# A bias added to four transposed chunks in one instruction, and a gate's mix issued one iteration later

## The chip, the cores and the metric

The kernel runs on one core of a Trainium2 chip. The metric is the device time of one execution in microseconds. A core has five engines that run side by side, each through its own list of instructions in order: TensorE (PE in the profile; its weight loads are shown apart as PEld), VectorE (DVE), ScalarE (ACT), GpSimd (POOL), and SyncE (SP), which here only issues transfers. A row whose engine ends in q (ACTq, DVEq) belongs to that engine's sequencer: a branch, a register read or the issue of a transfer.

## The reference, cut to what matters

The program is two layers. The first is a mixture of experts over tokens, and then a feed-forward network whose weights are chosen per sequence; the second mixes each token with the one before it, sends it to an expert and gates the result, and ends in a recurrent network. The stage that the change touches does the per-sequence network of layer one and the mixing and gate of layer two, for 32 sequences of 128 tokens with 512 features:

```python
sel = jnp.argmax(action_probs, axis=-1)          # one of 8 experts for each sequence
h = gelu(einsum('bsh,bhf->bsf', hidden_states, W1[sel]) + b1[sel][:, None, :])
reasoned = einsum('bsf,bfh->bsh', h, W2[sel]) + b2[sel][:, None, :]
x = ... hidden_states + 0.3 * (reasoned @ Wo + bo)
# second layer
xprev = concatenate([shift_state[:, None, :], x[:, :-1]], axis=1)
xk = x + (xprev - x) * time_maa_k                # goes to the experts
xr = x + (xprev - x) * time_maa_r                # goes to the gate
r = sigmoid(einsum('btd,ed->bte', xr, w_recept))
```

## The kernel before, in words

Everything is fp32 with each matrix operand held as two numbers, a high and a low part. `split(hi, lo, src)` makes them: a cast on ScalarE (L63) and a subtract on VectorE (L64). A product is then three matmuls, (high, high), (high, low) and (low, high), which `mm3` (L71) issues for each of four chunks of the contraction, so one product of 128 tokens by 512 columns is twelve matmuls.

The stage runs from about 862 us to 1466 us of the span. The sequences are sorted by expert, so that neighbours share weights. Weights are gathered on the GpSimd queue into three raw buffers (`fetch_w`, `rawB`, L851), with the biases of a sequence (L858) beside them; `split_w` (from L866) splits one of the four halves W1a, W2a, W1b, W2b in two pieces of 128x1024, at run time only where the expert differs from that of the sequence before. A branch on a register (L879) decides that, on ScalarE and on VectorE. In the profiled data the splits run around iterations 6, 15 and 16, 26, and always at 24, where the second part of the sorted list begins.

An iteration b carries three sequences at different depths. In program order it does:

- `up(b+1, "a")`: twelve matmuls into `pu`, and a copy `ue` on ScalarE (L1021).
- `turn_r(b-1)`: the result `ps` of the sequence before the current one is transposed in four chunks (`pr`, L1052) into a PSUM tile. Then, for each chunk, ScalarE adds the bias and writes the high part `rT` (L1057), and VectorE adds the bias and subtracts the high part to get the low one (L1058). These eight instructions alternate, since each low part needs its high part.
- `down(b, "a")` into `po`.
- In some iterations a `combine` of the layer's token experts (transposes `pth`, ScalarE's `o` at L744, VectorE's `xc` at L749); after iteration 17 also the choice of experts for the second part, `policy`.
- `bend(b+1, "a")`: four transposes `pt` (L1028), four gelu activations `hf` with the bias (L1031), and the split `hb`.
- `send_k(pair)`: four transposes `ptB` of the mixed `xk` (L1130), a copy `rows` (L1132), and a transfer by SP. This, and the other steps for a pair, happen in every other iteration.
- `up(b+1, "b")`, `send_k(pair + 1)`, `down(b, "b")` with the copy `ps` (L1045), `send_v(pair)` (twelve matmuls `pv` of the gate on `xr`, a copy `r` at L1142 and a transfer), `bend(b+1, "b")`, `send_v(pair + 1)`.
- After every second sequence `close(c)`: the output product `pb` for the pair (48 matmuls of 256 columns), and on VectorE the sum `x` (L1095), the difference `dx` (L1078) and the mix `xk` (L1080). GpSimd first puts the shifted-in row into `x` (L1071, `x<-condS`).
- Directly after `close(c)`, `mix_r(c)`: four instructions on VectorE that turn `dx` into the gate's mix in place (L1116), and its split into `xr` (a cast and a subtract of 128x1024).

Text such as "iteration 16" below means the stretch from `pu_16a`'s first matmul to that of the next sequence, by the number in the name of the `pu` that begins it. `close` thus stands at the end of an odd stretch and its VectorE work runs into the even one that follows.

The order in which each engine issues is fixed when the kernel is built: a scheduler places the instructions by readiness and by the program's order, and `tc.issue_after(ins)` keeps what is issued inside it behind an instruction on that instruction's engine. A tile belongs to a pool, and a new tile waits until the tile that had its buffer has been read. The pool `ps_tB` has two PSUM buffers, and `pr`, `pt`, `ptB` and `pth` take turns in it. `ps`, `dx`, `xk`, `xr`, `x1` and `rT` have one buffer each, the biases four, `hb` three.

Of the kernel before, what the change touches and what calls it, by code (L numbers as in the profile page):

```python
# [1 line left out]

# [6 lines left out]
F32 = mybir.dt.float32  # L9
# [5 lines left out]
AF = mybir.ActivationFunctionType  # L15
ALU = mybir.AluOpType
# [4 lines left out]
P = 128  # L21
D = 512
KD = D // P
NB = 32
# [16 lines left out]
BIAS = {"W1a": 0, "W1b": 1, "W2a": 2}  # L41
# [7 lines left out]
def tile_kernel(ctx: ExitStack, tc: tile.TileContext, a: dict, out: bass.AP):  # L49


    nc = tc.nc
# [4 lines left out]
    def shifted(pool, n, by=SHIFT, **kw):  # L57

        return pool.tile([P, n + (LINE if by == SHIFT else by)], FR, **kw)[:, by : by + n]

    def split(hi, lo, src):

        nc.scalar.copy(hi, src)  # L63
        return nc.vector.tensor_tensor(lo, src, hi.bitcast(F32), ALU.subtract).ins  # L64

    def mm3(ps, left, right, kd, start=True, stop=True):

# [78 lines left out]
    with ExitStack() as sa:  # L146
# [696 lines left out]
        raws, bcol, changed = {}, {}, {}  # L843
# [16 lines left out]
                        in_offset=bass.IndirectOffsetOnAxis(ap=idxb[:, b : b + 1], axis=0),  # L860
                    )

        def bias_of(kind, b, o):
            return bcol[b][:, BIAS[kind] * KD + o : BIAS[kind] * KD + o + 1]

        def split_w(i):  # L866

# [18 lines left out]
        with ExitStack() as s2:  # L886
# [15 lines left out]
            for g in range(h, NG):  # L902
                own = list(range((g - 1) * GB, g * GB)) if g > h else []
                for c in range(KF):
                    n = (2 if 0 < c < 3 else 0) if g == last else 1
# [43 lines left out]
    with ExitStack() as sb:  # L949
        kw = dict(reuse_waits="tile")  # L950
        lp = sb.enter_context(tc.tile_pool(name="lp", bufs=2, **kw))
        bp = sb.enter_context(tc.tile_pool(name="bp", bufs=1, **kw))
# [11 lines left out]
        PB = 2  # L964
        HF = F1 // 2

        def weight_b(name):
            pair = wb.tile([P, 2, KD, D], FR, tag=name, name=f"{name}_hl")
            flat = pair.rearrange("p h k n -> p h (k n)")
            given = a[name].rearrange("p k n -> p (k n)")  # L970
            for q, tag in enumerate(("dx", "xk")):
                s = bass.ts(q, KD * D // 2)
                raw = bp.tile([P, KD * D // 2], F32, tag=tag, name=f"raw_{name}{q}")
                nc.sync.dma_start(out=raw, in_=given[:, s])
                split(flat[:, 0, s], flat[:, 1, s], raw)
            return pair

        seqs, end_p = {}, None
# [13 lines left out]
        rTs, xks, xrs = {}, {}, {}  # L992

        def fetch_hid(b):
            if b < NB:
                hid_raw[b] = lp.tile([P, KD, P], F32, tag="hid", name=f"hidB_{b}")
                nc.sync.dma_start(out=hid_raw[b].rearrange("p k q -> p (k q)"), in_=by_seq(hid_d, b))
# [4 lines left out]
        def fetch_xh(c):  # L1002
            if c < NB // PB:
                xs[c] = lp.tile([P, PB, KD, P], F32, tag="x", bufs=1, name=f"xB_{c}")
                for j in range(PB):
                    nc.sync.dma_start(
                        out=xs[c][:, j].rearrange("p k q -> p (k q)"), in_=by_seq(xh_d, c * PB + j)
                    )

        def split_hid(b):  # L1010
            if b < NB:
                raw = hid_raw.pop(b)
                hid_hl[b] = lp.tile([P, 2, KD, P], FR, tag="hidhl", name=f"hidhl_{b}")
                split(hid_hl[b][:, 0], hid_hl[b][:, 1], raw)

        def up(b, half):
            w = ws["W1" + half]
            pu = ps_u.tile([P, HF], F32, tag="u", name=f"pu_{b}{half}")
            mm3(pu, lambda h, k: hid_hl[b][:, h, k, :], lambda h, k: w[:, h, k, :], KD)
            ues[b, half] = rp.tile([P, HF], F32, tag="ue", name=f"ue_{b}{half}")  # L1020
            nc.scalar.copy(ues[b, half], pu)  # L1021
# [13 lines left out]
        def down(b, half):  # L1035
            w, hb = ws["W2" + half], hbs.pop((b, half))
            if half == "a":
                pos[b] = ps_o.tile([P, D], F32, tag="o", name=f"po_{b}")
            mm3(
                pos[b], lambda h, k: hb[:, h, k, :], lambda h, k: w[:, h, k, :], KD,  # L1040
                half == "a", half == "b",
            )
            if half == "b":
                pss[b] = rp.tile([P, D], F32, tag="ps", bufs=1, name=f"ps_{b}")
                nc.scalar.copy(pss[b], pos.pop(b))  # L1045

        def turn_r(b):
            c, j = divmod(b, PB)
            ps = pss.pop(b)
            pt = ps_t.tile([P, KD, P], F32, tag="t", name=f"pr_{b}")  # L1050
            for o in range(KD):
                nc.tensor.transpose(pt[:, o, :], ps[:, bass.ts(o, P)], ident)  # L1052
            if j == 0:
                rTs[c] = rTp.tile([P, 2, KD, PB * P], FR, tag="rT", name=f"rT_{c}")
            for o in range(KD):
                hi = rTs[c][:, 0, o, bass.ts(j, P)]
                done_a = nc.scalar.activation(hi, pt[:, o, :], AF.Identity, bias=bias_of("W2a", b, o))  # L1057
                done_v = nc.vector.scalar_tensor_tensor(  # L1058
                    rTs[c][:, 1, o, bass.ts(j, P)], pt[:, o, :], bias_of("W2a", b, o),
                    hi.bitcast(F32), ALU.add, ALU.subtract,  # L1060
                )
            return done_a.ins, done_v.ins

        def close(c, last=False):

# [46 lines left out]
        def mix_r(c, pool, tag):  # L1112

            _, dx, x1 = xks[c]
            for k in range(KD):
                nc.vector.scalar_tensor_tensor(  # L1116
                    dx[:, k], dx[:, k], maa_r[:, k : k + 1], x1[:, k, :, 1:], ALU.mult, ALU.add
                )
            if pool is not end_p:
                xrs[c] = pool.tile([P, 2, KD, PB, P], FR, tag=tag, name=f"xr_{c}")  # L1120
            else:
                xr = shifted(pool, 2 * KD * PB * P, LINE - SHIFT, tag=tag, name=f"xr_{c}")
                xrs[c] = xr.rearrange("p (h k b q) -> p h k b q", h=2, k=KD, b=PB)
            split(xrs[c][:, 0], xrs[c][:, 1], dx)
# [26 lines left out]
        def used():  # L1151
            nonlocal at
            split_w(at + AHEAD)
            at += 1

        for b in range(-1, NB + 1):
            c, j = divmod(b - 1, PB)
            if b + 1 < NB:
                up(b + 1, "a")
                used()  # L1160
                split_hid(b + 2)
                fetch_hid(b + 3)
            if 0 <= b - 1 < NB:
                r_done = turn_r(b - 1)
            if 0 <= b < NB:
                down(b, "a")
                used()
            if b == -1:
                fetch_xh(0)
            if b == 0:  # L1170
                wo0 = weight_b("Wo")
            if b == 1:
                wrec = weight_b("w_recept")

            late, step = divmod(b - 3, 3)
            if 0 <= late < GB and step == 0:
                get_o(NB - GB + late, cb, 1)
            if 0 <= late < GB and step == 2:
                combine(NB - GB + late, ps_t)
            if late == GB and step == 2:  # L1180
                policy(PARTS[0], NB, cb, ps_t)
            if b + 1 < NB:
                bend(b + 1, "a")

            pair = b - 3 if b % 2 and 0 <= b - 3 < NB - 2 else None
            if pair is not None:
                send_k(pair)
            if b + 1 < NB:
                up(b + 1, "b")
                used()  # L1190
            if late == GB and step == 2:
                sc.close()
                end_p = sb.enter_context(tc.tile_pool(name="end_p", bufs=1, **kw))
            if pair is not None:
                send_k(pair + 1)
            if b == NB:
                send_v(NB - 6)
            if 0 <= b < NB:
                down(b, "b")
                used()  # L1200
            if pair is not None and pair < NB - 6:
                send_v(pair)
            if b + 1 < NB:
                bend(b + 1, "b")
            if pair is not None and pair < NB - 6:
                send_v(pair + 1)
            if j == PB - 1 and 0 <= c < NB // PB:
                wo_done, k_done = close(c, b == NB)
                fetch_xh(c + 1)
                if c < NB // PB - 2:  # L1210
                    mix_r(c, bp, "xr")
                elif c == NB // PB - 2:
                    mix_r(c, end_p, "xr")

        with tc.issue_after(wo_done):
            send_v(NB - 5)
# [13 lines left out]
    with ExitStack() as sd:  # L1230
# [97 lines left out]
        for p in range(NPC):  # L1328
# [6 lines left out]
            if p == NPC - 12:  # L1335
                c = first_p.tile([P, D], F32, tag="c0", name="c_0")
                nc.sync.dma_start(out=c, in_=a["in_c"].partition_broadcast(P))
                cT = first_p.tile([P, 2, KD, P], FR, tag="cT0", name="cT_0")
                pt = ps_t.tile([P, KD, P], F32, tag="t", name="ptC_0")
# [25 lines left out]
    with sf:  # L1365
# [135 lines left out]
        ps, wx = {}, {}  # L1501
# [15 lines left out]
        bias = {n: load_row("b" + n, D, keep_p) for n in "cif"}  # L1517

        cT_next = cT
        for t in range(NB):  # L1520
# [15 lines left out]
            c = new_c(t, v, c)  # L1536
            ps = {}
# [58 lines left out]
        for n, (g, o) in enumerate(units):  # L1596
            if g == NG - 1:
                to_z(o)
                src = pos.pop(o)
                h = yp.tile([P, GT], F32, tag="y", name=f"hF_{g}_{o}")  # L1600
            else:
                src = h = zos[g, o]
# [99 lines left out]
```

## Time and profile before

| what | value |
|---|---|
| time, median of 3 runs | 2541.81 us (2541.47, 2541.81, 2545.81) |
| the profiled execution | 2535.17 us |
| its span, first to last instruction | 2533.5 us |
| mean granted TensorE clock | 0.988 |
| TensorE busy | 2460.9 us (97%) |
| VectorE busy | 1332.4 us (53%) |
| ScalarE busy | 1064.2 us (42%) |
| the stage of the change, 862 to 1466 us: TensorE busy | 590.31 of 604.00 us |

The profile is of one execution, and its own time stands above beside its span. "Busy" is time in which an engine executes something that computes. A row of the groups gives the line, the engine, the operation, what is written from what, the shape and count, then the busy time and the mean of one in ns, and then the idle time of that engine just before the group, with what ended it. In the chain of waits each engine's wait is put down to the instruction that released it. A "granted clock" below 1.00 means that TensorE's matmuls ran slower in part of the stretch.

### The profile page before, as it was taken

The numbers are of one execution on the slowest core, as the hardware profiler recorded it, in microseconds if no ns is written. First come the engines' busy times: TensorE is split into PE (matmuls) and PEld (weight loads), VectorE is DVE, ScalarE is ACT, GpSimd is POOL, SyncE is SP. The second block draws the span as 40 slices with busy tenths as digits, with TensorE's granted clock in tenths as the row PEclk, the third lists the DMA queues.
The fourth block names the chain that finished last, engine by engine and source line by source line (L and its number), as shares of the span: only waits on it lengthen the run. The fifth ranks groups of instructions, "written<-read, shape, count | busy, mean of one in ns | idle before, by whom it ended". The sixth has DMA issues, their size and how long they took to land. (4 is left out here: it accounts for less than half of the span.)

```text
span 2533.5 us, 37051 instructions
## 1 busy us (share of the span) xinstructions
PE 2460.9 (97%) x13044; PEld 2077.8 (82%) x13044; DVE 1332.4 (53%) x2341; ACT 1064.2 (42%) x1935; POOL 428.5 (17%) x460
## 2 busy tenths in 40 slices
PE   8999999999999899999999999999999999999996
PEld 6788899887887787888887889999978888888885
DVE  7796645556557344445444477667643333333336
ACT  5445533443224445445455466666532222222214
POOL 1000022222223223322322110000010000000003
PEclk9999999999999999999999999999999999999998
DMA  5545544557555333332243387776441111111027
GB/s 181 162 132 172 172 156 152 169 184 254 180 177 169 113 97 126 113 116 99 85 143 116 105 283 238 230 229 224 152 162 42 38 38 38 38 42 46 25 78 267
DMA packets 193116, 351.11 MB, mean 139 GB/s; under 512 B 37472, under 2 KB 72336, under 8 KB 189856
## 3 DMA queue, kind: packets, MB, share of 16 engines
q1 hardware_dynamic: 141504, 244.42, 29.0%
q0 software_dynamic: 36160, 74.90, 10.0%
q10 hardware_dynamic: 15264, 29.37, 3.3%
q8 instruction: 108, 1.77, 0.3%
q14 instruction: 80, 0.66, 0.1%
HBM read 373.94 MB, written 88.13 MB: 182 GB/s over the span
## 5 line engine op out<-in xcount | busy, mean ns | idle before, releaser
L64 DVE TENSOR_TENSOR wD<-rawD,wD 128x1024 fp32r<-128x1024 f32 x128 | 156.5, 1229 | 77.7 <-ACT wD L63 77.7
L71 PE MATMUL p<-xhl,swu 128*128 128x512 f32 x768 | 189.0, 397 | 5.3 <-ACT xhl L63 5.3
L71 PE MATMUL p<-xhl,kept_u 128*128 128x512 f32 x768 | 185.6, 397 | 0.7 <-DVE kept_u L64 0.7
L71 PEld LDWEIGHTS phD<-xe,wD 128*128 128x128 f32 x1536 | 184.7, 189 | 1.8 <-ACT xe L63 0.6
L71 PE MATMUL phD<-xe,wD 128*128 128x256 f32 x1536 | 185.7, 281 | 0.5 <-ACT xe L63 0.5
L71 PE MATMUL poD<-wD,hD 128*128 128x512 f32 x768 | 181.3, 392 | 0.0
L71 PEld LDWEIGHTS p<-xhl,swu 128*128 128x128 f32 x768 | 144.7, 191 | 36.5 <-ACT xhl L63 5.6
L71 PEld LDWEIGHTS p<-xhl,kept_u 128*128 128x128 f32 x768 | 143.3, 190 | 30.5 <-DVE kept_u L64 1.1
L71 PEld LDWEIGHTS poD<-wD,hD 128*128 128x128 f32 x768 | 141.9, 188 | 28.4
L63 ACT CAST wD<-rawD 128x1024 fp32r<-128x1024 f32 x128 | 133.2, 1047 | 53.6 <-PE poD L71 31.0
L266 POOL DMA_INDIRECT xg<-in_x_rows_dram,blk_t x71 | 67.5, 951 | 461.3 <-PE ptx L276 257.4
L1384 POOL DMA_INDIRECT y<-res_d,gat_i x32 | 32.2, 1005 | 575.0 <-DVE r L1403 496.2
L71 PE MATMUL pur<-r,xb 128*128 x852 | 117.8, 287 | 0.9 <-ACT xb L63 0.4
L71 PE MATMUL por<-r,hbr 128*128 x426 | 116.3, 407 | 1.2 <-ACT hbr L63 1.1
L64 DVE TENSOR_TENSOR xb<-ptx,xb 128x512 fp32r<-128x512 f32 x71 | 49.1, 691 | 115.3 <-ACT xb L63 113.7
L71 PEld LDWEIGHTS pur<-r,xb 128*128 128x128 f32 x852 | 104.9, 189 | 2.0 <-ACT xb L63 0.9
L71 PE MATMUL acc<-kept_d,as 128*128 128x512 f32 x384 | 96.1, 400 | 5.1 <-DVE as L64 3.1
L71 PE MATMUL poF<-z,wo_hl 128*128 128x512 f32 x384 | 96.5, 399 | 0.0
L71 PE MATMUL ps_f<-wf_hl,z 128*128 128x512 f32 x384 | 96.4, 399 | 0.0
L71 PE MATMUL ps_c<-wc_hl,z 128*128 128x512 f32 x384 | 94.9, 395 | 0.7 <-issue 0.7
L71 PE MATMUL acc<-swd,as 128*128 128x512 f32 x384 | 95.0, 392 | 0.0
L71 PE MATMUL pb<-rT,Wo_hl 128*128 128x256 f32 x768 | 94.6, 281 | 0.0
(1014 smaller groups left out, 5040.0 us busy)
## 6 DMA issues: line engine op xcount, KB each, us to landing
rawD<-in_w_key_dram SPq DMA_DIRECT2D x64, 512.0 KB
rawD<-in_w_value_dram SPq DMA_DIRECT2D x64, 512.0 KB
swr<-in_sw_dram SPq DMA_DIRECT2D x120, 256.0 KB
o_d<-obr SPq DMA_DIRECT2D x71, 256.0 KB
xraw<-in_x_dram SPq DMA_DIRECT2D x32, 256.0 KB
rraw<-in_rw_dram SPq DMA_DIRECT2D x32, 256.0 KB
xc<-in_x_dram SPq DMA_DIRECT2D x32, 256.0 KB
hid_d<-o ACTq DMA_DIRECT2D x32, 256.0 KB
```

Of the source, the lines that this page charges most:

```text
L63: nc.scalar.copy(hi, src)
L64: return nc.vector.tensor_tensor(lo, src, hi.bitcast(F32), ALU.subtract).ins
L71: done = nc.tensor.matmul(ps, lhsT=left(hl, k), rhs=right(hr, k), start=start and k + n == 0, stop=stop and 3 * k + n == last,)
L266: nc.gpsimd.indirect_dma_start(out=xg[i], out_offset=None, in_=a["x_rows"], in_offset=bass.IndirectOffsetOnAxis(ap=blk_t[:, i : i + 1], ax ...
L1384: nc.gpsimd.indirect_dma_start(out=y, out_offset=None, in_=res_d, in_offset=bass.IndirectOffsetOnAxis(ap=gat_i[:, b : b + 1], axis=0),)
```

## The change

Two things are edited, and a helper is added for the second. In `turn_r` the bias is added to all four transposed chunks by one VectorE instruction, which reads the PSUM tile and writes over the `ps` tile, whose content has been transposed by then; the bias operand is the sequence's four columns, each broadcast over 128 tokens. One `split` of the sum then writes the high and low parts of all four chunks. `split` now records its two instructions in `last_split`.

The mix for the gate, `mix_r(c)`, is no longer issued right after `close(c)` but in the following iteration after `bend(b+1, "a")`, and kept behind that bend's split `hb` on both ScalarE and VectorE. For one pair, at the end of the stage, no sequence is left to bend, and no such order is asked for. The last pair's mix stays where it was, after the loop.

```diff
     def split(hi, lo, src):
-        nc.scalar.copy(hi, src)
-        return nc.vector.tensor_tensor(lo, src, hi.bitcast(F32), ALU.subtract).ins
+        first = nc.scalar.copy(hi, src).ins
+        done = nc.vector.tensor_tensor(lo, src, hi.bitcast(F32), ALU.subtract).ins
+        last_split[:] = first, done
+        return done
+
+    last_split = []
+
+    @contextmanager
+    def behind(both):
+        with tc.issue_after(both[0]), tc.issue_after(both[1]):
+            yield
...
-        def bias_of(kind, b, o):
-            return bcol[b][:, BIAS[kind] * KD + o : BIAS[kind] * KD + o + 1]
+        def bias_of(kind, b, o, n=1):
+            return bcol[b][:, BIAS[kind] * KD + o : BIAS[kind] * KD + o + n]
...
-            for o in range(KD):
-                hi = rTs[c][:, 0, o, bass.ts(j, P)]
-                done_a = nc.scalar.activation(hi, pt[:, o, :], AF.Identity, bias=bias_of("W2a", b, o))
-                done_v = nc.vector.scalar_tensor_tensor(
-                    rTs[c][:, 1, o, bass.ts(j, P)], pt[:, o, :], bias_of("W2a", b, o),
-                    hi.bitcast(F32), ALU.add, ALU.subtract,
-                )
-            return done_a.ins, done_v.ins
+            rT = ps.rearrange("p (k q) -> p k q", k=KD)
+            bias = bias_of("W2a", b, 0, KD).unsqueeze(2).to_broadcast([P, KD, P])
+            nc.vector.tensor_tensor(rT, pt, bias, ALU.add)
+            s = bass.ts(j, P)
+            split(rTs[c][:, 0, :, s], rTs[c][:, 1, :, s], rT)
+            return tuple(last_split)
...
             if b + 1 < NB:
                 bend(b + 1, "a")
 
+            if j == 0 and 0 < c < NB // PB:
+                with behind(last_split) if b + 1 < NB else nullcontext():
+                    mix_r(c - 1, end_p if c == NB // PB - 1 else bp, "xr")
+
...
                 wo_done, k_done = close(c, b == NB)
                 fetch_xh(c + 1)
-                if c < NB // PB - 2:
-                    mix_r(c, bp, "xr")
-                elif c == NB // PB - 2:
-                    mix_r(c, end_p, "xr")
```

More of the change, by code (lines that the diff above doesn't have):

```diff
@@ L1 @@
-from contextlib import ExitStack, nullcontext
+from contextlib import ExitStack, contextmanager, nullcontext
 import concourse.bass as bass
```

## The prediction
> **What bounds the kernel now.** I read the busy table and the chain's shares first, then cut the stage into its iterations with the table of windows, then asked for TensorE's waits and last for one iteration's timeline.
>
> ```profile
> PE 2460.9 (97%) x13044; PEld 2077.8 (82%) x13044; DVE 1332.4 (53%) x2341; ACT 1064.2 (42%) x1935; POOL 428.5 (17%) x460
> PE 41%; DVE 1%; DMA 1%; ACT 0%; issue 0%; POOL 0%; POOLq 0%; ACTq 0%; DVEq 0%
> ```
>
> PE carries the chain; VectorE (DVE) and ScalarE (ACT) are half idle. Work removed from them is worth only the PE gaps that it closes. The stage runs from 862 to 1466 us; its windows (busy us per engine, then granted clock, DMA share, GB/s) are the stage, an odd iteration, iterations 22, 6, 16 and 26:
>
> ```profile
> 862.00:1466.00 604.00, 590.31 (x3178) 499.35 (x3179) 279.30 (x540) 308.24 (x693) 174.75 (x173) 0.99 0.35 111
> 1235.27:1253.20 17.93, 17.93 (x109) 15.81 (x108) 4.29 (x10) 7.67 (x19) 5.10 (x5) 1.00 0.07 17
> 1253.22:1272.51 19.29, 18.95 (x94) 15.39 (x93) 9.76 (x19) 9.48 (x22) 6.06 (x6) 1.00 0.68 197
> 943.20:966.80 23.60, 20.99 (x99) 17.12 (x98) 16.05 (x28) 13.63 (x27) 8.84 (x9) 0.93 0.57 171
> 1137.20:1160.00 22.80, 20.49 (x94) 16.67 (x93) 14.30 (x23) 13.44 (x26) 5.49 (x6) 0.93 0.45 152
> 1327.50:1350.50 23.00, 20.55 (x95) 16.60 (x94) 14.17 (x23) 13.25 (x26) 6.28 (x6) 0.93 0.46 150
> ```
>
> PE idles 604.00 − 590.31 = 13.7 us in the whole stage. Odd iterations are full. An even one holds six groups of twelve matmuls (po to pt_16a below: 2.85 us each) and five turns of four transposes (pr to po: 0.35), 18.7 us if PE never waits; 22 loses 0.6 of its 19.29, and 6, 16 and 26, where an expert's weights change, over 4 each (6 has one turn more for the combine, 19.0). The waits (total, times, longest, us) name the cause:
>
> ```profile
> PE pt_6a L1028 <- ACT o L744: 2.6, 1, 2.6
> PE ptB L1130 <- ACT hf_26a L1031: 2.4, 1, 2.4
> PE ptB L1130 <- ACT hf_16a L1031: 2.3, 1, 2.3
> PE pt_15a L1028 <- DVEq L879: 2.0, 1, 2.0
> PE ptB L1130 <- ACT hf_30a L1031: 0.7, 1, 0.7
> PE ptB L1130 <- ACT hf_22a L1031: 0.3, 1, 0.3
> ```
>
> ptB and pt take turns in a pool of two PSUM buffers, so ptB needs the buffer that the gelus hf have read. In iteration 16's timeline (start, us, idle before) ACT reaches them late:
>
> ```profile
> 1139.99 0.60 PE L1052 MATMUL pr<-ident,ps 128*128 128x128 f32 x4
> 1140.34 3.01 PE L71 MATMUL po<-wB_W2a,hb_15a 128*128 128x512 f32 x12
> 1143.19 0.60 PE L1028 MATMUL pt_16a<-ident,ue_16a 128*128 128x128 f32 x4
> 1143.43 1.05 ACT L63 CAST xr<-dx 128x1024 fp32r<-128x1024 f32 x1 [2.39 <-DVE dx L1116]
> 1144.38 1.99 ACT L63 CAST wB_W2a<-rawB 128x1024 fp32r<-128x1024 f32 x2
> 1146.28 0.36 ACT L1057 ACTIVATE rT<-pr,b 128x128 fp32r<-128x128 f32 x1
> 1146.54 1.13 ACT L1031 ACTIVATE hf_16a<-pt_16a,b 128x128 f32<-128x128 f32 x4
> 1147.73 1.11 PE L1130 MATMUL ptB<-ident,xk 128*128 128x128 f32 x4 [2.31 <-ACT hf_16a L1031]
> ```
>
> The gate's cast stands ahead of the gelus and waits 2.39 us for DVE's mix; the gelus pay for it. Yet pv, the gate's reader, comes 5 us later (in iteration 22 xr is complete at 1261.43, pv starts at 1266.58). The move spends that slack.
>
> **What the Trainium skill says.** "TensorE: Matmul & The Clock Gate", its table of specifications: ScalarE's and VectorE's queues are strict FIFO. The trace agrees: hf_16a stands behind a cast it does not need. Same page, Part 1: the clock gate halves TensorE after an idle window of about 3.4 us that runs freely. The trace half agrees: iterations 6, 16 and 26 show clock 0.93 after waits of 2.6, 2.3 and 2.4 us, shorter than that window; 2.0 us in iteration 15 left it at 1.00. "VectorE: DVE Perf Modes", the tier table: fp32 tensor_tensor, and any with a PSUM operand, runs at 1×. The trace agrees: such an add of 128x512 from PSUM (v_c<-ps_c,bc) takes 692 ns.
>
> **The change, part by part.** Per sequence the turned result cost, by these two groups (count, busy, mean ns, idle before), 4 × 370 = 1.48 us of ACT and 4 × 349 = 1.40 of DVE, alternating, so some 3.1 us as a chain:
>
> ```profile
> L1057 ACT ACTIVATE rT<-pr,b 128x128 fp32r<-128x128 f32 x128 | 47.3, 370 | 35.3 <-DVE rT L1058 29.0 <-PE pr L1052 5.0
> L1058 DVE SCALAR_TENSOR_TENSOR rT<-pr,b,rT 128x128 fp32r<-128x128 f32 x128 | 44.7, 349 | 66.4 <-ACT rT L1057 56.4 <-ACTq L879 8.7 <-DVEq L879 0.4
> ```
>
> After: one DVE add from PSUM, 0.69 us (v_c's row), one ACT cast of 128x512, 0.62 (hb's cast), one DVE subtract, 0.69: a chain of 2.0 us. Over 32 sequences ACT saves 32 × (1.48 − 0.62) = 27.5 us, DVE 32 × (1.40 − 1.38) = 0.6. Neither bounds, so directly it is worth nothing. What matters: pr's PSUM buffer is free after the add instead of after eight instructions. The broadcast bias operand (stride 0) is not in the trace; 0.69 to 0.9 us, I take 0.69, since a tensor_tensor at 1× has no tier to lose. The ps tile is held 1.3 us longer; its next writer comes at the iteration's end.
>
> The mix's instructions (four of L1116, 1.67 us; cast 1.05; subtract 1.23) are the same, issued after hb_a's cast and subtract, an iteration after close. It reads dx and x1, which stay put. On POOL, x<-condS now waits longer for the mix to release x1, and the gathers of weights behind it in that queue with it; the next close is an iteration away and weights are fetched three steps ahead, so the cover is a full odd iteration of 18 us. SP issues the same transfers (x_d, xk_d, hidB, xB), with v_d's after pv as before. Both queues: 0. The ordering adds a wait: behind xr's cast on ACT stand ps's copy and hf_b, behind its subtract on DVE hb_b's subtract. ps is read by pr 6 us later and hb_b by po the iteration after, so up to some 3 us there cost PE nothing but pv itself.
>
> I replayed the new order of instructions with these durations, offsets from pu_22a's start in **ordinary even iterations**: xk done 4.2, add to 4.9, rT's cast to 5.55, gelus 6.6 to 7.75, first rows copy 8.25, hb cast 8.8, hb subtract 9.5; dx to 11.4; xr's cast 11.45 to 12.5; its subtract to 13.8. PE reaches ptB at 6.3 (pr's buffer free at 4.9), the second ptB at 9.5, pv at 12.7: 0.2 after its cast. The third matmul of pv, first reader of xr's low half, is due at 13.36 and waits to 13.8: 0.44, against some 0.55 lost now. Seven such (4, 8, 10, 14, 20, 22, 28): −0.1 each, **−0.7**. What is late next is thus xr itself.
>
> **Changing experts.** 16: no ptB wait, but W1b's or W2a's split (cast pair 1.99, subtract pair 2.36) still stands ahead of xr: its cast ends 1.27 us after PE wants it and its subtract 0.6 more, 1.9 for 4.1 now, **−2.2**. In 6 the mix stands behind the combine and W1b: pt_6a waits 0.65 for the add, ptB 0.72 for the combine's o, pv 2.45 for xr, 3.8 for 4.5 lost now. In 26: ptB 0.74, pv 2.4 and 0.6, 3.7 for 4.3. Whether waits of 2.4 us again halve the clock is unknown; it cost 16 the 4.1 us lost less 2.3 waited for ptB and 0.4 of small gaps, 1.4: −0.7 or +0.7 each, I take **0**. 15: pt_15a waits 0.35 for the add instead of 1.98, **−1.65**.
>
> **The rest.** 12: pt_12a's wait on the combine goes, −0.5 (the waits name 0.5). 30: hf_30a's 0.7 goes and no pv follows there, −0.7. 18: pv now waits 1.2 for an xr behind the policy's DVE work, 0.4 lost now, **+0.8**. 24: the second part's first split of W2a is unconditional and delays xr, +0.5. Tail, where the last pb follows turn_r closely and needs rT's low half after one 0.69 us subtract instead of four 0.35 ones already under way: +0.2, an estimate. Odd iterations: 0, rT is wanted by pb 13 us later.
>
> Sum: −0.7 − 2.2 − 1.65 − 0.5 − 0.7 + 0.8 + 0.5 + 0.2 = **−4.3 us**. The profiled execution took 2535.17 us (span 2533.5 and 1.67 around it) and would take 2530.9; it lies 6.64 below the median shown, 2541.81, to which I apply the difference: **2537.5**.
>
> **Rivals.** (1) *xr is always in time*: every gap named closes and the half-rate stretches with it: 4.5 + 4.1 + 4.3 in three iterations less 3 left, plus 1.65 and 7 × 0.2, −12 us: 2530. For: xr's lateness is 0.4 us in my walk, within its error. Against: DVE has 9 to 16 us of work in an even iteration, in one queue. (2) *The wait is only exchanged*: ptB's 0.3 becomes pv's 0.4, 2.4 becomes 2.4, and 15 alone gains: 2541. For: the new stalls come out nearly as large as the old. (3) *Slower: xr becomes the bound*. pv sits at 12.7; if the mix starts 1 us later than I walked (hb's subtract waits for an ACT that runs late through rows copies), each of 14 gated pairs adds 1 us less the 0.5 saved, +7, and in 6 and 26 the wait passes 3 us and halves the clock, +1.4 each, less 2 from 15 and 16: +8, 2550. It decides from the point where xr's low half lands over 1 us after pv's third matmul is due. For: five instructions now stand ahead of it. Against: ACT is freed of 0.86 us per sequence. That the edit does nothing is excluded: the order of instructions differs on three engines.
>
> **How the numbers follow.** About 0.2%, 5.1 us, is what a measurement of this kernel can tell from no change. My walk 0.53 (about 2535 to 2541; 0.26 of it beyond −5.1, 0.27 within), rival 1 0.24 (all faster), rival 2 0.06 (same), rival 3 0.17 (slower). So faster 0.50, same 0.33, slower 0.17. The range runs from rival 1, 2530, to half way into rival 3, 2546.
>
> **What would show it.** Right: TensorE's list of waits loses hf_16a, hf_26a and pt_15a, pv <- xr appears at 0.3 to 0.5 in ordinary pairs and 2 in 6 and 26; the turned result is three rows near 0.69, 0.62, 0.69; iteration 22 stays near 19.2 us and 16 falls from 22.8 to 20.6. Wrong: even iterations above 19.8 us (rival 3), or clock 1.00 in 6 and 26 with no wait over 1 us (rival 1).

## The result, and the profile after

The changed kernel takes 2533.39 us (median; 2529.52 to 2539.18), the kernel before, run beside it, 2540.91 (2534.97 to 2545.81). The ratio is 0.9974, 95% interval 0.9967 to 0.9981: a gain of 4.8 to 8.4 us. The forecast of 2537.5, a gain of 4.3, lies just short of that; its range of 2530 to 2546 holds the time. The profiled execution took 2532.29 us (span 2530.6) against 2535.17, only 2.9 less. That pair of spans is a poor measure: a second profile of the kernel before, told below, has a span of 2542.6 with the same stage inside. So the stage is measured from `pu_0a`'s first matmul to `pu_31a`'s: 572.43 us before, **567.46 after, 5.0 less**. That lies within the interval of the runs; the medians of the runs differ by 7.5, and where the other 2.5 us lie is not shown.

The page's busy line and the shares of the chain:

```profile
PE 2462.6 (97%) x13044; PEld 2079.5 (82%) x13044; DVE 1334.5 (53%) x2277; ACT 1042.0 (41%) x1839; POOL 419.3 (17%) x460
PE 43%; DVE 1%; DMA 1%; issue 0%; POOL 0%; ACT 0%; POOLq 0%; DVEq 0%; ACTq 0%
```

ACT lost 22.2 us of busy time and DVE gained 2.1, and neither shows in the time. The table of windows (stretch, length, busy us of PE, PEld, DVE, ACT and POOL, granted clock, DMA share, GB/s) has the stretch from `pu_0a` to `pu_31a`, then iterations 6, 16, 22 and 26:

```profile
847.69:1415.15 567.46, 552.82 (x2952) 465.83 (x2950) 262.46 (x441) 275.40 (x571) 167.00 (x177) 0.98 0.36 113
943.48:967.88 24.40, 21.43 (x98) 17.05 (x97) 16.94 (x27) 13.40 (x24) 7.64 (x9) 0.93 0.64 204
1135.27:1155.06 19.79, 19.30 (x95) 15.45 (x94) 14.38 (x21) 12.51 (x23) 5.72 (x6) 1.00 0.55 174
1249.14:1268.23 19.09, 19.06 (x94) 15.51 (x93) 9.75 (x17) 8.74 (x19) 5.31 (x6) 1.00 0.66 210
1323.66:1347.04 23.38, 20.90 (x94) 16.45 (x93) 14.13 (x21) 12.60 (x23) 6.36 (x6) 0.93 0.47 148
```

Iteration 16 lost 3.0 us and runs at full clock; 22 lost 0.2; 6 and 26 are longer than before. TensorE's waits in the stage (total, times, longest; the one for `ue_0b` at its entry, 7.9 us before and 7.5 after, left out) say why:

```profile
PE pv L81 <- ACTq L889: 4.4, 3, 2.0
PE pt_6a L1038 <- DVE ps L1068: 0.6, 1, 0.6
PE ptB L1139 <- DVE ps L1068: 0.5, 1, 0.5
PE ptB L1139 <- ACT o L754: 0.5, 1, 0.5
PE pv L81 <- ACT xr L63: 0.4, 2, 0.2
PE pv L81 <- DVE xr L64: 0.3, 1, 0.3
```

No gelu `hf` is waited for any more, and the transposes wait at most 0.6 us, for the new add or the combine's `o`. The new wait is pv's, 1.91 us in 6 and 1.99 in 26. ACTq names the branch behind the cast; the timeline of iteration 26 (start, us, engine, what, idle before) shows what held the cast itself:

```profile
1333.65 0.69 DVE L64 TENSOR_TENSOR hb_26a<-hf_26a,hb_26a 128x512 fp32r<-128x512 f32 x1 [1.60 <-ACT hb_26a L63]
1334.26 0.88 DVE L1125 SCALAR_TENSOR_TENSOR dx<-dx,maa_r_sb,x 128x256 f32<-128x256 f32 x2
1335.05 2.35 DVE L64 TENSOR_TENSOR wB_W1b<-rawB,wB_W1b 128x1024 fp32r<-128x1024 f32 x2
1337.32 0.88 DVE L1125 SCALAR_TENSOR_TENSOR dx<-dx,maa_r_sb,x 128x256 f32<-128x256 f32 x2
1338.23 1.04 ACT L63 CAST xr<-dx 128x1024 fp32r<-128x1024 f32 x1 [1.23 <-DVE dx L1125]
1339.33 1.07 PE L81 MATMUL pv<-w_recept_hl,xr 128*128 128x512 f32 x2 [1.99 <-ACTq L889]
1340.59 3.63 PE L81 MATMUL pv<-w_recept_hl,xr 128*128 128x512 f32 x10
```

The mix starts behind hb's subtract, and W1b's split, 2.35 us, falls into its middle. Then the ten matmuls of pv take 3.63 us, against 2.60 in iteration 22: the granted clock was 0.50 from 1340 to 1342 us and 0.53 in the microsecond after, then 1.00 again. The new way of turning the result costs, by the groups (busy, mean ns, idle before):

```profile
L1068 DVE TENSOR_TENSOR ps<-pr,b 128x512 f32<-128x512 f32 x32 | 22.0, 687 | 32.4 <-PE pr L1062 32.1 <-DVEq L889 0.2
L63 ACT CAST rT<-ps 128x512 fp32r<-128x512 f32 x32 | 19.9, 621 | 41.6 <-DVE ps L1068 41.6
L64 DVE TENSOR_TENSOR rT<-ps,rT 128x512 fp32r<-128x512 f32 x32 | 22.2, 693 | 20.2 <-ACTq L889 16.5 <-ACT rT L63 3.7
```

### The profile page after: what moved, and what is told of

It reads as the page before. It is cut to its first block, busy times and chain, and to the rows that moved or that the text cites. A ratio compares the mean times of both kernels' runs of the same rounds, so it can differ in the third digit from the quotient of the medians.

```text
span 2530.6 us, 36870 instructions
## 1 busy us (share of the span) xinstructions
PE 2462.6 (97%) x13044; PEld 2079.5 (82%) x13044; DVE 1334.5 (53%) x2277; ACT 1042.0 (41%) x1839; POOL 419.3 (17%) x460
## 5 line engine op out<-in xcount | busy, mean ns | idle before, releaser
L81 PE MATMUL pv<-w_recept_hl,xr 128*128 128x512 f32 x384 | 99.9, 408 | 5.5 <-ACTq L889 4.4
```

The costliest lines, as they stand in the source:

```text
L81: done = nc.tensor.matmul(ps, lhsT=left(hl, k), rhs=right(hr, k), start=start and k + n == 0, stop=stop and 3 * k + n == last,)
```

## The experiments

The question was which of the two edits made the gain, and by what. The table gives each kernel's time from `pu_0a` to `pu_31a`, the mean of seven ordinary even iterations (4, 8, 10, 14, 20, 22, 28), single iterations, and the ratio of the runs to the kernel before. Each number is the difference between two starts in a timeline.

| kernel | stage | ordinary | 6 | 15 | 16 | 18+19 | 26 | ratio (95%) |
|---|---|---|---|---|---|---|---|---|
| before | 572.4 | 19.25 | 23.51 | 20.60 | 22.80 | 37.98 | 23.01 | 1 |
| before, second profile | 572.6 | 19.25 | 23.58 | 20.77 | 22.84 | 38.00 | 23.03 | |
| after (add, mix behind hb) | 567.5 | 19.09 | 24.40 | 18.39 | 19.79 | 39.09 | 23.38 | 0.9974 (0.9967 to 0.9981) |
| add alone, mix in old place | 565.3 | 19.03 | 23.58 | 20.06 | 19.63 | 38.18 | 22.58 | 0.9965 (0.9953 to 0.9976) |
| mix behind hb alone | 579.5 | 19.35 | 25.55 | 19.76 | 25.16 | 39.03 | 24.73 | 1.0022 (1.0013 to 1.0030) |
| add, mix moved but free | 556.2 | 18.72 | 20.64 | 20.17 | 18.74 | 38.06 | 19.44 | 0.9938 (0.9925 to 0.9950) |
| old turn, mix moved but free | 571.2 | 19.07 | 23.12 | 24.19 | 20.51 | 38.24 | 22.82 | 0.9994 (0.9984 to 1.0003) |
| add, mix behind hb on ACT only | 557.3 | 18.72 | 21.80 | 19.87 | 18.74 | 38.81 | 19.47 | 0.9946 (0.9933 to 0.9959) |
| add, mix behind hb on DVE only | 567.0 | 19.09 | 24.42 | 18.39 | 19.78 | 39.11 | 22.36 | 0.9978 (0.9966 to 0.9990) |
| after, experts never change | 556.8 | 19.08 | 19.39 | 18.39 | 19.07 | 39.10 | 19.08 | 0.9948 (0.9933 to 0.9962) |
| copy and eight, mix moved but free | 556.8 | 18.72 | 22.85 | 20.66 | 18.71 | 37.89 | 19.45 | 0.9951 (0.9939 to 0.9962) |
| copy and eight, mix in old place | 564.9 | 18.98 | 23.16 | 21.18 | 20.30 | 38.24 | 21.03 | 0.9969 (0.9959 to 0.9978) |

One iteration has to be set apart: 1, at the stage's entry, took 20.7 to 22.6 us, and not in the order of the edits. In the add alone, the kernel whose experts never change and the two copy kernels its mean granted clock was 0.84 and it took 20.74 to 21.81; in the others 0.77, and 22.03 to 22.64. Of the two copy kernels' 556.8 and 564.9, some 2 and 0.7 us are owed to that, and 0.7 each of the 565.3 of the add alone and the 556.8 without a change of experts. All but before have one profile, so differences of a microsecond between stages are not pressed.

**The kernel before once more.**

> The kernel before once more, for a second profile of it. Theory (the profiled execution of before was a lucky one: its 2535.17 us lies 5.7 below the median of its runs, that of after only 1.1 below): another execution shows more iterations with a granted clock below 1.00 after waits near 2 us, or longer waits, in the stage or outside, and a span of 2536 to 2541. Rival (the 5.7 us lie outside the span or the profile shortens every execution): the same span within 1 us and the same stage, 627.6.

The span is 2542.6 us, 9.1 longer than in the first profile. The stage reproduces to 0.2 us, every even iteration to 0.1. The extra time is elsewhere: `pu_0a` starts at 852.44 us instead of 847.30, the stretch from `pu_31a` to the next stage's first matmul, `phD`, takes 56.34 instead of 55.20, and 2.6 more comes after it. Iterations 6, 15, 16 and 26 show the same granted clock as in the first profile (0.93, 1.00, 0.93, 0.93). So neither text is right: up to `phD` it is 629.0 us, near the rival's 627.6, but the span is longer than either said. The first profile, 2535.17 us, was near the shortest of the runs beside it (2534.97 to 2545.81), and this one, 2544.26, is longer than all beside it (2532.42 to 2541.98): the stage repeats, the rest does not, and so a difference of 2.9 us between two spans says little.

**The single add alone.** The mix goes back to its place after the output product:

```diff
-            if j == 0 and 0 < c < NB // PB:
-                with behind(last_split) if b + 1 < NB else nullcontext():
-                    mix_r(c - 1, end_p if c == NB // PB - 1 else bp, "xr")
...
                 fetch_xh(c + 1)
+                if c < NB // PB - 2:
+                    mix_r(c, bp, "xr")
+                elif c == NB // PB - 2:
+                    mix_r(c, end_p, "xr")
```

> The bias is added to all four chunks at once, the mix stays right after the output product. Theory (both parts are needed: the single add frees pr's PSUM buffer early, the move takes the gate's cast from in front of the gelus): ordinary even iterations stay near 19.2 us, since the add stands behind the mix on VectorE and ptB waits 0.3 for it; 16 and 26 keep over 1 us of waits; the stage from pu_0a to the first phD takes 625 to 626 us (627.6 before, 623.7 with both parts), ratio 0.998 to 0.9995. Rival (the bias part alone carries the gain, the move is only an exchange): 623.5 us or less, ratio 0.997, as with both.

The theory fell: the add alone gains 7.1 us in the stage, as much as both edits together or more (622.0 us to the first phD, the rival's side). Its lead of 2.1 us over the changed kernel, 0.7 of it from iteration 1, is not clear in the runs, whose intervals overlap. The timeline of its iteration 22:

```profile
1250.89 1.67 DVE L1125 SCALAR_TENSOR_TENSOR dx<-dx,maa_r_sb,x 128x256 f32<-128x256 f32 x4
1252.48 0.68 DVE L1068 TENSOR_TENSOR ps<-pr,b 128x512 f32<-128x512 f32 x1
1252.59 1.05 ACT L63 CAST xr<-dx 128x1024 fp32r<-128x1024 f32 x1 [2.35 <-DVE dx L1125]
1253.21 0.66 PE L1139 MATMUL ptB<-ident,xk 128*128 128x128 f32 x4
1253.75 0.62 ACT L63 CAST rT<-ps 128x512 fp32r<-128x512 f32 x1
1254.28 1.14 ACT L1041 ACTIVATE hf_22a<-pt_22a,b 128x128 f32<-128x128 f32 x4
```

The gate's cast still stands ahead of the gelus and still waits 2.35 us. It no longer matters: ptB takes the buffer of `pr`, which the add has just read, and does not need that of the gelus.

**The move alone.** `turn_r` with its eight instructions, the mix behind hb:

```diff
-            rT = ps.rearrange("p (k q) -> p k q", k=KD)
-            bias = bias_of("W2a", b, 0, KD).unsqueeze(2).to_broadcast([P, KD, P])
-            nc.vector.tensor_tensor(rT, pt, bias, ALU.add)
...
+            for o in range(KD):
+                hi = rTs[c][:, 0, o, bass.ts(j, P)]
+                done_a = nc.scalar.activation(hi, pt[:, o, :], AF.Identity, bias=bias_of("W2a", b, o))
...
```

> The mix is made an iteration later behind hb's split, the result is still turned with eight alternating instructions. Theory: pr's buffer comes free only near 6.9 us into an ordinary even iteration, ptB is due at 6.3, so it waits 0.6 and pv waits up to 0.4 more: even iterations 19.3 to 19.6, a stage of 626 to 628 us, ratio 0.999 to 1.001. Rival (the move alone carries the gain): 19.1 us, a stage below 625, ratio 0.997 to 0.998.

Slower, by 7.1 us in the stage (634.5 to the first phD), and by more than the theory said. Ordinary iterations are as expected (19.35), but 6, 16 and 26 rise by 1.7 to 2.4 us. The timeline of iteration 16:

```profile
1147.66 2.36 DVE L64 TENSOR_TENSOR wB_W2a<-rawB,wB_W2a 128x1024 fp32r<-128x1024 f32 x2 [1.37 <-ACT wB_W2a L63]
1149.94 0.34 DVE L1069 SCALAR_TENSOR_TENSOR rT<-pr,b,rT 128x128 fp32r<-128x128 f32 x1
1150.34 1.11 PE L1141 MATMUL ptB<-ident,xk 128*128 128x128 f32 x4 [3.37 <-DVE rT L1069]
```

The last of the eight instructions, 0.34 us long, stands behind a weight's split of 2.36, and holds pr's buffer until then; ptB waits 3.37.

**The move without its order.** One line of the changed kernel:

```diff
-                with behind(last_split) if b + 1 < NB else nullcontext():
+                with nullcontext():
```

> The changed kernel with the mix in its new place in program order, but not held behind hb's split: the scheduler now puts the mix before W1b's split and hb's split on VectorE, and the gate's cast right behind the gelus on ScalarE. Theory (in 6 and 26 pv waits 2 us because W1b's subtract stands between mix and gate): pv's waits vanish, 6 and 26 fall from 24.4 and 23.4 to about 20.5, 18 with 19 gains back 1 us, the stage takes 616 to 618 us (623.7), ratio to before 0.994 to 0.9955. Rival (the order behind hb is what keeps ScalarE free; without it rows and hb come late and ptB or pt waits again): 623 us or more, ratio 0.997 or above.

The theory held, and its size was too small: 556.2 us, 11.2 less than the changed kernel, and to the first phD 610.6 where 616 to 618 was expected. Pv waits for nothing any more. The window of iteration 26 is at full clock:

```profile
1317.88:1337.32 19.44, 18.96 (x94) 15.49 (x93) 14.31 (x21) 12.63 (x23) 5.53 (x6) 1.00 0.42 121
```

Iterations 6 and 26 came out as expected or better (20.64 and 19.44, for 20.5), and so did the ratio. The ordinary iterations gave 0.4 each, which had not been counted. This version has the lowest ratio of all; its interval lies clear of those of the changed kernel and of the add alone. So the move is worth something too, where no order holds the mix back.

**The old turn with the free mix.** The same line as above, in the kernel with the move alone.

> The mix in its new place in program order without the order behind hb, and the result still turned with eight alternating instructions. Theory (pr's PSUM buffer is what counts, and only the single add frees it early; here the fourth low part still stands behind the gate's mix and W2a's subtract on VectorE): ordinary even iterations 19.2 to 19.4, 16 above 22 with ptB or the gelus waiting, pu_0a to pu_31a 570 to 576 us (572.4 before, 556.2 with the single add and the free mix), ratio 0.999 to 1.002. Rival (the free place of the mix is the gain, with either way of turning): 558 to 562 us, ratio 0.995 to 0.997.

571.2 us and a ratio of 0.9994: no gain without the add. The sum is the theory's, its detail is not. Ordinary iterations fell to 19.07, iteration 16 fell to 20.51, while 15 rose to 24.19, where pt_15a waits 3.1 us.

**Which engine's order costs.** `behind` orders on both engines; here on one:

```diff
-                with behind(last_split) if b + 1 < NB else nullcontext():
+                with tc.issue_after(last_split[0]) if b + 1 < NB else nullcontext():
```

> The changed kernel with the mix held behind hb's cast on ScalarE only; on VectorE the scheduler is free. Theory (what the order behind hb costs is VectorE's half: it lets W1b's subtract and hb's subtract go ahead of the mix): 556 to 559 us from pu_0a to pu_31a, as without any order (556.2), 26 at 19.4, ratio 0.994 to 0.9955. Rival (the cast's place on ScalarE matters as much): 562 us or more, ratio 0.996 to 0.9975.

and the same with `last_split[1]`:

> The changed kernel with the mix held behind hb's subtract on VectorE only. Theory (the VectorE half is the whole cost): 566 to 569 us from pu_0a to pu_31a, as with both (567.5), 6 and 26 above 23, 18 with 19 near 39, ratio 0.997 to 0.9985. Rival (ScalarE's half is the cost): below 562 us, ratio below 0.996.

Both as the theory said: 557.3 with ScalarE's half, 567.0 with VectorE's. Iteration 26 of the second missed its number in an instructive way. Its timeline, to be read beside that of the changed kernel:

```profile
1340.23 0.73 PE L81 MATMUL pv<-w_recept_hl,xr 128*128 128x512 f32 x2 [2.02 <-ACTq L889]
1341.49 2.60 PE L81 MATMUL pv<-w_recept_hl,xr 128*128 128x512 f32 x10 [0.32 <-DVEq L889]
```

The wait is the same, 2.02 for 1.99, but here the clock was not halved: 2.60 for ten matmuls instead of 3.63, which is the 1.0 us between 22.36 and 23.38.

**No change of experts.**

```diff
-            nc.vector.tensor_tensor(same[:, 1:], srow[:, 1:], srow[:, : nb - 1], ALU.is_equal)
+            nc.vector.tensor_tensor(same[:, 1:], srow[:, 1:], srow[:, : nb - 1], ALU.is_ge)
```

> The changed kernel, instruction for instruction, with the comparison of neighbours' experts always true: weights are loaded and split only for the first sequence and for the first of the second part, so the other sequences use a wrong expert's weights. Theory (the 2 us that pv waits in 6 and 26 is W1b's split standing ahead of the mix): 6 falls from 24.4 to about 19.5, 26 from 23.4 to 19.1, 16 from 19.8 to 19.2, 24 stays at 19.5, 18 with 19 stays at 39; pu_0a to pu_31a about 558 us (567.5). Rival (the mix is late in these iterations for another reason, transfers or the combine): 6 and 26 stay above 22, 564 us or more.

As expected in every iteration named: 19.39, 19.08, 19.07, 19.52 in 24, 39.10 in 18 and 19. The waits that are left from 870 to 1480 us, those of the next stage left out (pb's is the tail's):

```profile
PE pv L81 <- ACTq L889: 0.4, 1, 0.4
PE pb L81 <- DVE rT L64: 0.2, 1, 0.2
PE pv L81 <- ACT xr L63: 0.2, 1, 0.2
```

So pv's waits of 2 us come with the weights' splits. This kernel takes away all four of them and their transfers; that it is W1b's, ahead of the mix, is shown by the timeline of 26 and by the kernel with ScalarE's order alone, whose source lacks only VectorE's half of the order: there VectorE makes the mix before W1b's split, and 26 takes 19.47.

**What in the single add does it.** It frees pr's buffer early, and it shortens the work in two queues. A copy out of PSUM separates these:

```diff
-            nc.vector.tensor_tensor(rT, pt, bias, ALU.add)
...
+            nc.vector.tensor_copy(rT, pt)
+            for o in range(KD):
+                hi = rTs[c][:, 0, o, bass.ts(j, P)]
+                done_a = nc.scalar.activation(hi, rT[:, o, :], AF.Identity, bias=bias_of("W2a", b, o))
+                done_v = nc.vector.scalar_tensor_tensor(
+                    rTs[c][:, 1, o, bass.ts(j, P)], rT[:, o, :], bias_of("W2a", b, o),
+                    hi.bitcast(F32), ALU.add, ALU.subtract,
+                )
```

> The mix in its new place without the order behind hb; VectorE first copies pr out of PSUM in one instruction, and the eight alternating instructions then work from the copy in ps. So pr's buffer comes free as early as with the single add, but the chain of eight stays in both queues. Without any order the single add took 556.2 us from pu_0a to pu_31a and the old turn from PSUM 571.2. Theory (the buffer that comes free early is the larger part of the gain): 558 to 563 us, no ptB waiting over 0.5 for the turn outside 6 and 26, the rest lost where the gelus stand behind the chain; ratio 0.9945 to 0.997. Rival (the time that the eight instructions take in the queues is the larger part): 566 us or more, ratio above 0.998.

> The same copy and eight instructions with the mix right after the output product, as in the kernel before. The single add in this place took 565.3 us from pu_0a to pu_31a, the old turn 572.4. Theory (the buffer): 565.5 to 568.5, ptB's waits on the gelus of 16 at 1.4 and of 26 below 1; ratio 0.997 to 0.9985. Rival (the queues): 571 or more, ratio 0.999 to 1.001.

Both came out at, or just below, the theory's lower end. The groups of the first show that the old work is all there, and a copy on top:

```profile
L1070 ACT ACTIVATE rT<-ps,b 128x128 fp32r<-128x128 f32 x128 | 41.2, 393 | 42.2 <-DVE ps L1067 34.0 <-DVE xk L1093 8.0
L1071 DVE SCALAR_TENSOR_TENSOR rT<-ps,b,rT 128x128 fp32r<-128x128 f32 x128 | 38.1, 350 | 7.9 <-ACT rT L1070 7.5 <-DVEq L889 0.2
L1067 DVE COPY ps<-pr 128x512 f32<-128x512 f32 x32 | 22.0, 688 | 30.9 <-PE pr L1062 30.6
```

With 32 instructions of 0.69 us *more* than before, this kernel is within 2.5 us of the one with the single add (556.8 for 556.2, 1.9 of it owed to iteration 1); in the mix's old place the two are equal within 1 us, though single iterations differ by more, both ways (26: 21.03 for 22.58, with the granted clock at 1.00 for 0.92; 15: 21.18 for 20.06). So the add gains by freeing the buffer. A third buffer in `ps_tB`, which would test the same from the other side, was not run. What the shorter chain is worth can be read in iteration 6 of the free kernels alone, 22.85 with the copy for 20.64: ptB waits 1.14 us for `o` instead of 0.47, and the eleven matmuls of `pu_6b` behind it take 4.21 us for 2.81, with the granted clock at 0.53 from 952 to 954 us. Some 0.7 us is thus the chain's own, and the rest came with the clock.

## Why the prediction was right or wrong

The range held the time, and the sum of the stage, −4.5 without the tail, compares with a measured −5.0. That closeness is in part luck: in the table the ordinary iterations, 15, 16 and 30 came out 2.0 us better than forecast, and 6, 26, 12 and 18 with 19 came out 1.7 worse. Its terms (us, from the iterations' lengths):

| step | forecast | measured |
|---|---|---|
| seven ordinary iterations | −0.7 | −1.2 |
| 15 | −1.65 | −2.2 |
| 16 | −2.2 | −3.0 |
| 6 / 26 | 0 / 0 | +0.9 / +0.4 |
| 12 / 30 | −0.5 / −0.7 | −0.4 / −0.9 |
| 18 with 19 | +0.8 | +1.1 |
| 24 | +0.5 | +0.45 |
| `pu_31a` to the first phD | +0.2 | not separable: 55.2 and 56.3 in two profiles of before, 56.3 after; the wait it names is there, pb's for `rT`, 0.2 |

- **The replay of the order was good to 0.2 us in iteration 22.** There pv starts 12.81 us in (forecast 12.7), xr's cast ends at 12.36 (12.5), its subtract at 13.63 (13.8). The unknown price of the broadcast bias was rightly taken as none: 687 ns. The waits of pv for xr, 0.3 to 0.5 in ordinary pairs, do not show in the list: in 22 two transposes of `pt_22b` stand between pv's second and third matmul. The time is lost all the same, 19.09 us for 18.72 in ordinary iterations of the free kernel. By that, 18.7 us without waits is right, though six groups of 2.85 and five turns of 0.35 make 18.85.
- **The step that failed is the attribution: "The move spends that slack".** The prediction took the gelus, late behind the gate's cast, for what had to be cured, and the move for the cure. The add cures it alone, by giving ptB another buffer (−7.1 us), with the cast still ahead of the gelus. The move as written, with its order behind hb, costs 7.1 us alone, where ptB then waits for the turn, and some 2 on top of the add, since hb and W1b go ahead of the mix; without that order it is worth 9.1 on top of the add (565.3 to 556.2). The prediction had named the buffer as what matters, and priced W1b ahead of the mix in 6 and 26, but summed both edits as one replay, where a gain and a loss met.
- **"Whether waits of 2.4 us again halve the clock is unknown".** They did in 6 and 26 of the changed kernel, after waits of 1.91 and 1.99, at about 1.0 us in 26. With the forecast's −0.7 or +0.7 the upper end was the right one for 6.
- **In 16 the wait was overestimated**: 1.9 us for xr, measured 0.18 and 0.31. W2a's split went ahead of the gelus and not between mix and gate.
- **"Both queues: 0" missed something in 15.** In the add-alone and the free kernel the gate's copy r waits 4 us there on ACT, in the free one by the trace for the transfer of `rows`, with W1a's split behind it; in the changed kernel it waits 0.7. There W1b's gather leaves POOL 14.4 us after `pu_14a`, after a wait of 2.1 us that the trace puts down to VectorE's queue, and in those two at 13.3 and 13.0. That the later gather leaves `rows` more of the memory's time fits, but no run isolates it.
- **The rivals.** That the wait is only exchanged is true for 6 and 26. Rival 3's sign is that of the move without the add (ratio 1.0022), but there ptB waits for the turn (6.3 us in six waits) more than pv for xr. Rival 1, xr always in time, is the kernel with the free mix, at −16 us in the stage even larger than said (its terms add up to 13, not 12).

The Trainium skill's strict FIFO ("TensorE: Matmul & The Clock Gate", table of specifications) is what all of this rests on, and the traces agree: in the move alone a 0.34 us instruction held a PSUM buffer over 3 us for what stood ahead of it. The same page's idle window of about 3.4 us (Part 1), that runs freely, fits in that two nearly equal waits, 1.99 and 2.02 us, met it differently, one halving the clock and one not; in length the waits are again shorter than the window stated, and here the measurement decides.

## What to carry to other kernels

When an operation reads a PSUM tile in many small steps on two engines, the tile's buffer is free only after the last of them, and that one can stand behind other work in its queue. One instruction that takes the whole tile out of PSUM can free it earlier, and here that paid even where it added work. Before moving work later, ask what is issued in its place: an order behind an urgent instruction also lets everything the scheduler likes go ahead, and here dropping the order was worth twice the whole change in the stage, 11.2 us to 5.0. Two edits made together should be timed apart, since one can hide the other's loss.

## What the runs showed of the hardware that was not expected

- A bias broadcast over 128 columns (stride 0) cost VectorE nothing that shows: 687 ns for the add of 128x512 from PSUM, against 688 for a plain copy of the same shape.
- The activation that adds the bias to 128x128 took 370 ns from PSUM and 393 from SBUF (means of 128 each). In the second kernel they follow each other and overlap, so that all 128 kept ScalarE busy for 41.2 us, against 47.3 in the first.
- After a wait of 1.99 us the granted clock was 0.50 for some 3 us, and the ten matmuls then took 3.63 us; after one of 2.02 us in the same place of another kernel it stayed at 1.00, and they took 2.60. In iteration 6 of the copy kernel with the free mix a wait of 1.14 us, with one of 0.58 shortly before it, was enough; with 0.47 in place of the 1.14 the clock stayed at 1.00. Two profiles of the kernel before agree in which of the iterations 6, 15, 16 and 26 the clock was lowered. What decides between two nearly equal waits is not shown.
